# Adjacency attention followed by a graph attention layer: when the second layer's steps are issued among the first layer's beats

## The chip, the cores and the metric

The kernel runs on one core of a Trainium2 chip. The time is the device time of one execution in microseconds (us); before the change it is 4539.56 us, the median of three runs (4534.59 to 4539.63). The engines are PE (matrix products), DVE (vector), ACT (activation functions), POOL (GpSimd) and SP (which only issues transfers). Each has its own queue of instructions and they meet through semaphores.

## The reference

Two layers over x of shape 8 x 2048 x 256 (batch, node, feature) and one adjacency matrix of 2048 x 2048, all in float32.

```python
# layer 0: attention in 4 heads of 64, softmax within each chunk of 256 keys
scores = einsum('bhnd,bhjcd->bhnjc', q, kc) / sqrt(64)
scores = clip(scores, -10, 10); scores = where(mask == 0, -10, scores)
ctx = einsum('bhnjc,bhjcd->bhnd', softmax(scores, axis=-1), vc)   # the 8 chunks are summed
out = layernorm_affine(ctx @ Wo.T + bo + x)
x = layernorm(x + out)
# layer 1: graph attention, one head
Wh = x @ W;  s_i = Wh @ a1;  s_j = Wh @ a2
e = where(mask | eye, leaky_relu(s_i + s_j, 0.2), -inf)
x = layernorm(x + elu(softmax(e, axis=-1) @ Wh))
```

So layer 0 needs a softmax sum for each of 8 chunks, and layer 1 of a batch needs layer 0 of all of that batch's nodes.

## The kernel before, in words

**Layer 0.** Queries are taken in blocks of 512 (4 blocks, `ib`, in each of 8 batches, `b`) and keys in chunks of 256 (8 chunks, `j`). One (b, ib, j) is a pair of beats; there are 256 pairs, 32 for each batch. A beat (`half` 0 or 1) covers 128 keys: PE makes the scores `sc` of 4 heads (line 989) in two PSUM tiles, DVE caps and masks them in place (line 1006, "the cap"), ACT takes the exponential into `e` (line 1015). One pair later PE makes the values `u` from `e` and `v` (`values`, line 895), ACT copies them to `un` (line 1049), and the softmax sums follow (`sums`, line 909): ACT copies a sum to `ds` (line 921), a transfer gathers it as `dc`, DVE takes its reciprocal (line 926), and two more transfers (`rd`, `r`) spread it over the partitions. `scaled` multiplies `un` by `r` on DVE (line 939, or 937 for the first chunk), and POOL adds it to `ctxT` (line 940). In what follows this is "the product with the reciprocal". `inverses` puts `inverse`, `spread` and `scaled` on an agenda for given beats.

**Layer 1.** For each batch and query block there are 16 steps, one for each 128 keys: ACT `low` (line 723), DVE `leaky` and `edges` (lines 727 and 732), ACT exponential (`weights`, line 736) with a running sum `acc` on POOL (line 747), and PE `product` into the PSUM tile `us` (line 757), of which there is one. After step 15 ACT copies `us` to `hx` (line 784). A step's tile `w` comes from a pool of six. 28 blocks, those of batches 0 to 6, are of this form; batch 7 runs after the main loop in a form of its own (line 772).

**Which steps run where.** Layer 1 of a batch runs beside layer 0 of the next. A generator, `prelude`, makes `Wh`, the row maxima (two half-maxima, line 442, in each pair or more) and the row `ab` for each block; `blocks_done` and `ab` decide when a block may start. When layer 1 is under way (`together`), a pair does this: in its first beat `leaky` and `edges`, then all the values, then `weights`; in its second beat `take_lows` starts new steps and `end_beat` issues the products. Steps are metered by a credit of 1.5 for each beat (1.3 in the last batch), so three start in a pair whatever block they belong to. In such pairs two transfers on POOL's queue add the `e` tiles of the second beat to those of the first (line 1043), and the sums, taken a pair later, read one set of tiles instead of two. Other pairs ("quiet") take the sums at once, over both.

**Finish pieces.** `fin` (layer 0: output projection `po`, line 361, then two layer norms and a transpose) and `fin1` (layer 1: reciprocal, ELU and layer norm) are generators that advance one piece in a beat, from the list `fins`; the k and v projections of the next batch are in it too. `prelude` is in the list `ahead`.

**Order.** Instructions are issued in the order in which the program is written, by each engine. In the second beat of a pair with layer 1, `end_beat` issues the products, a piece of `ahead`, the pieces of `fins`, and a piece of `ahead` again; then what is due on the agenda. `inverses(p, 0)` puts the reciprocal at the end of the very beat in which the sums are made, and `scaled` two beats later (three in quiet pairs). The first 32 pairs, without layer 1, use lag 1 and four.

Of the kernel before, what the change touches and what calls it, by code (L numbers as in the profile page):

```python
# [28 lines left out]
def tile_adj_attention__then__gat(  # L29
# [36 lines left out]
    B, N, F = x.shape  # L66
# [3 lines left out]
    NT = N // P  # L70
    IB = 512
    NIB = N // IB
    TPB = IB // P
    NPAIR = H // 2
    NCH = N // CHUNK
# [268 lines left out]
    fins = []  # L344
# [352 lines left out]
    total = B * NIB * NCH  # L697

    def layer1():

        for b in range(B):
            st = states[b]
            for ib in range(NIB):
                while ib not in st["ab"] or beat < st["ab"][ib][0]:
                    yield None
                mks = [mask_block(1, ib, 0, f"{b}_{ib}_0")]
                block = {"b": b, "ib": ib, "ab": st["ab"].pop(ib)[1], "wh": st["wh"], "sj": st["sj"], "mks": mks}
                for c in range(NT):
                    if c == 3:
                        mks.append(mask_block(1, ib, 1, f"{b}_{ib}_1"))  # L710
                    yield Step(block, c)

    class Step:
# [11 lines left out]
        def leaky(self):  # L725
            k, c = self.k, self.c
            nc.vector.scalar_tensor_tensor(  # L727
                self.w, k["ab"][:, 0, :], k["sj"][:, 0, c : c + 1], self.w, ALU.add, ALU.max
            )

        def edges(self):
            nc.vector.tensor_tensor(self.w, self.w, self.k["mks"][self.c // HT][:, self.c % HT, :], ALU.min)  # L732
# [78 lines left out]

    l1 = layer1()
    l1_live = True
    ahead = [prelude(b) for b in range(B - 1)] + [last_prelude(B - 1)]

    flight = {"low": [], "leaked": [], "edged": [], "weighted": []}
    kept = []
    FROM = {"leaky": "low", "edges": "leaked", "weights": "edged"}  # L820
    agenda = {}
    beat = 0
    credit = 0.0
    RATE, LAST_RATE = 1.5, 1.3

    def l1_open():
        return any(flight.values())
# [1 line left out]
    def at(when, fn):  # L829
        agenda.setdefault(when, []).append(fn)  # L830

    def take_lows(rate, most=2.0):

        nonlocal l1_live, credit
        credit = min(credit + rate, most)
        while l1_live and credit >= 1.0 and len(set(sum(flight.values(), kept))) < 6:
            s = next(l1, False)
            if s is False:
                l1_live = False
            elif s is None:  # L840
                break
            else:
                credit -= 1.0
                flight["low"].append(s)
                s.low()

    def advance(stage, to):

        for s in flight[FROM[stage]]:
            getattr(s, stage)()  # L850
        flight[to] += flight[FROM[stage]]
        flight[FROM[stage]] = []

    def weights():
        advance("weights", "weighted")

    def leaky():
        advance("leaky", "leaked")

    def edges():  # L860
        advance("edges", "edged")

    def end_beat(products, half=None):

        if beat < 2 * NIB * NCH or beat >= 2 * total:
            for fn in agenda.pop(beat, []):
                fn()
        if products:
            for s in flight["weighted"]:
                s.product()  # L870
            flight["weighted"] = []
        for gens in {None: (ahead, fins), 0: (fins,), 1: (ahead, fins, ahead)}[half] if beat < 2 * total else (fins, ahead):
            for g in list(gens):
                if next(g, g) is g:
                    gens.remove(g)
        for fn in agenda.pop(beat, []):
            fn()


    first_m0 = two.tile([P, HT, IB], I8, tag="mask0", name="mk0_0_0_0")  # L880
# [36 lines left out]
    def inverses(p, lag):  # L917


        ds = one.tile([P, IB], F32, tag="ds", name=f"ds{p['name']}")  # L920
        nc.scalar.copy(ds, p.pop("m"))  # L921
        p["dc"] = two.tile([P, IB // DH], F32, tag="dc", name=f"dc{p['name']}")
        nc.sync.dma_start(out=p["dc"], in_=ds.rearrange("(h m) (n w) -> h m n w", m=DH, n=DH)[:, 0, :, :])

        def inverse():
            nc.vector.reciprocal(p["dc"], p["dc"])  # L926
            p["rd"] = dram3.tile([H, IB], F32, tag="rd", name=f"rd{p['name']}")
            nc.sync.dma_start(out=p["rd"].rearrange("h (m w) -> (h m) w", m=DH), in_=p["dc"])

        def spread():  # L930
            p["r"] = two.tile([P, IB], F32, tag="r", name=f"r{p['name']}")
            nc.sync.dma_start(out=p["r"], in_=p["rd"].unsqueeze(1).to_broadcast([H, DH, IB]))

        def scaled():
            r2 = p["r"].unsqueeze(1).to_broadcast([P, 2, IB])
            if p["j"] == 0:
                nc.vector.tensor_mul(p["ctxT"], p["un"], r2)
            else:
                nc.vector.tensor_mul(p["un"], p["un"], r2)  # L939
                nc.gpsimd.tensor_add(p["ctxT"], p["ctxT"], p["un"])  # L940
            if p["j"] == NCH - 1:
                ctx_done[p["b"], p["ib"]] = beat
            if p["j"] == NCH - 3:
                fins.append(fin(p["b"], p["ib"], p["ctxT"]))

        at(beat + lag, inverse)
        at(beat + lag, spread)
        at(beat + (2 if p["added"] or beat >= 2 * total else 3 + lag), scaled)

    prev = None  # L950
    unsummed = []
    mk0 = {}
    for J in range(total + 1):
        b, ib, j = J // (NIB * NCH), J // NCH % NIB, J % NCH
        live = J < total
# [3 lines left out]
        for half in range(2):  # L959
            c = 2 * j + half  # L960
            if live:
# [6 lines left out]
                if c % HT == 1:  # L968
                    n = (b * NIB + ib) * 2 + c // HT + 1
                    nb, nib, nhf = n // (2 * NIB), n // 2 % NIB, n % 2  # L970
                    if 0 < nb < B:
                        mk0[nb, nib, nhf] = mask_block(0, nib, nhf, f"{nb}_{nib}_{nhf}")
            early = J < NIB * NCH
            rate = RATE if b < B - 1 else LAST_RATE
            if half == 0:
                together = prev is not None and live and l1_open()
            if not together:
                weights()
                waiting, flight["low"] = flight["low"], []
                take_lows(rate)  # L980
                new, flight["low"] = flight["low"], waiting
                leaky()
                flight["low"] = new
            scs = []
            if live:
                for hp in range(NPAIR):
# [11 lines left out]
            if half == 0:  # L998
                for p in unsummed:
                    sums(p)  # L1000
                    inverses(p, 0)
                unsummed = []
            if live:
                cap = mk[:, c % HT, :].unsqueeze(1).to_broadcast([P, 2, IB])
# [2 lines left out]
                for hp in range(NPAIR):  # L1007
# [6 lines left out]
                    )  # L1014
                    nc.scalar.activation(e, scs[hp], AF.Exp)  # L1015
                    cur["es"].append(e)
            if not together:
                edges()
            elif half == 0:
                for s in flight["low"]:  # L1020
                    s.leaky()
                    s.edges()
                flight["edged"] += flight["low"]
                flight["low"] = []
            else:
                take_lows(2 * rate, 3.5)

            if prev is not None:
                if half == 0:
                    prev["un"] = three.tile([P, 2, IB], F32, tag="un", name=f"un{prev['name']}")  # L1030
                    if not together:
                        sums(prev)
                        inverses(prev, 1 if early else 0)
                parts = (0, 1) if together and half == 0 else (half,) if not together else ()
                ms = [ps_m.tile([P, IB], F32, tag="m", name=f"u{prev['name']}_{part}") for part in parts]
                for i in range(2):
                    for part, m in zip(parts, ms):
                        values(prev, part, m, i)
                    if together and half == 0 and i == 1:


                        for hp in range(NPAIR):
                            nc.gpsimd.dma_start(  # L1043
                                out=prev["es"][hp], in_=prev["es"][NPAIR + hp], accum_op=ALU.add
                            )
                        prev["added"] = True
                        unsummed.append(prev)
                for part, m in zip(parts, ms):
                    nc.scalar.copy(prev["un"][:, part, :], m)  # L1049
            if together and half == 0:  # L1050
                weights()

            end_beat(half == 1 or not together, half if together else None)
            if half == 1:

                if live and j == NCH - 2 and J + 2 < total:
# [5 lines left out]
        prev = cur if live else None  # L1062

    while agenda or fins or ahead or l1_live or l1_open():
        weights()
        waiting, flight["low"] = flight["low"], []
        take_lows(1.0)
        new, flight["low"] = flight["low"], waiting
        leaky()
        flight["low"] = new  # L1070
        edges()
        end_beat(True)
        beat += 1


# [42 lines left out]
```

## Time and profile before

| | |
|---|---|
| median of three runs | 4539.56 us |
| the profiled execution | 4546.43 us, of which the span of instructions is 4544.3 us |
| busy PE, DVE, ACT, POOL | 3998.4, 3357.3, 2586.8, 2019.7 us |
| scores on PE (line 989) | 1090.6 us busy, mean 645 ns, x4096 |
| caps on DVE (line 1006) | 1205.1 us busy, mean 1220 ns, x1024 |
| layer 1 products on PE (line 757) | 858.5 us busy, mean 395 ns, x3584 |
| granted PE clock | 0.958 of full speed |

One matrix product in float32 appears as two records, so 4096 records of scores are 2048 products. Busy times of overlapping records count once. A wait is given as the engine that idled, the line that it idled before, and what ended the idle time. Waits of PE's weight loads (PEld) and of its matmuls (PE) for one thing are the same wait seen twice.

### The profile page before, as it was taken

The numbers are of one execution on the slowest core, as the hardware profiler recorded it, in microseconds if no ns is written. First come the engines' busy times: TensorE is split into PE (matmuls) and PEld (weight loads), VectorE is DVE, ScalarE is ACT, GpSimd is POOL, SyncE is SP. The second block draws the span as 40 slices with busy tenths as digits, with TensorE's granted clock in tenths as the row PEclk, the third lists the DMA queues.
The fourth block names the chain that finished last, engine by engine and source line by source line (L and its number), as shares of the span: only waits on it lengthen the run. The fifth ranks groups of instructions, "written<-read, shape, count | busy, mean of one in ns | idle before, by whom it ended". The sixth has DMA issues, their size and how long they took to land. (4 is left out here: it accounts for less than half of the span.)

```text
span 4544.3 us, 59493 instructions
## 1 busy us (share of the span) xinstructions
PE 3998.4 (88%) x21845; PEld 1897.5 (42%) x21845; DVE 3357.3 (74%) x4530; ACT 2586.8 (57%) x3842; POOL 2019.7 (44%) x1203
## 2 busy tenths in 40 slices
PE   9889988899889988899888988989888998888667
PEld 3223334453344433454334543445434444244446
DVE  5876578766788657886578775886768866787777
ACT  5555556565555655665556654556655665555446
POOL 0222335554356433655346553555525554355520
PEclk9999999999999999999999999999999999999889
DMA  5554235553455434654356543555435654455521
GB/s 161 180 166 134 77 113 129 132 130 104 136 133 140 115 105 124 156 131 107 105 129 154 141 93 108 142 145 138 103 107 133 152 133 108 135 138 130 150 75 56
DMA packets 301125, 573.86 MB, mean 126 GB/s; under 512 B 90273, under 2 KB 125345, under 8 KB 299937
## 3 DMA queue, kind: packets, MB, share of 16 engines
q1 hardware_dynamic: 257344, 411.71, 29.8%
q0 software_dynamic: 43488, 158.35, 18.3%
q8 instruction: 171, 2.80, 0.3%
q14 instruction: 122, 0.99, 0.1%
HBM read 340.66 MB, written 68.88 MB: 90 GB/s over the span
## 5 line engine op out<-in xcount | busy, mean ns | idle before, releaser
L1006 DVE SCALAR_TENSOR_TENSOR sc<-sc,mk 128x1024 f32<-128x1024 f32 x1024 | 1205.1, 1220 | 560.7 <-PE sc L989 529.2
L1015 ACT ACTIVATE e<-sc 128x1024 f32<-128x1024 f32 x1024 | 1033.5, 1024 | 849.2 <-DVE sc L1006 810.3
L989 PE MATMUL sc<-qT,kT 64*128 64x512 f32 x4096 | 1090.6, 645 | 173.0 <-ACT e L1015 172.3
L757 PE MATMUL us<-wh,w 128*128 128x256 f32 x3584 | 858.5, 395 | 157.9 <-ACT hx L784 87.4
L895 PE MATMUL u<-e,v 128*32 128x512 f32 x8192 | 965.9, 596 | 26.1 <-ACT ds L921 26.0
L940 POOL TENSOR_TENSOR ctxT<-ctxT,un 128x1024 f32<-128x1024 f32 x224 | 559.8, 2499 | 853.3 <-DVE un L939 832.0
L757 PEld LDWEIGHTS us<-wh,w 128*128 128x128 f32 x3584 | 682.7, 195 | 387.8 <-ACT w L736 171.3
L747 POOL TENSOR_TENSOR acc<-acc,w 128x512 f32<-128x512 f32 x392 | 612.1, 1561 | 195.6 <-ACT w L736 178.4
L989 PEld LDWEIGHTS sc<-qT,kT 64*128 64x128 f32 x4096 | 353.3, 192 | 763.2 <-ACT e L1015 386.7
L1043 POOL DMA_DIRECT2D e<-e x302 | 269.1, 1032 | 873.2 <-PE u L895 707.2
L895 PEld LDWEIGHTS u<-e,v 128*32 128x32 f32 x8192 | 239.0, 110 | 694.5 <-issue 499.4
L727 DVE SCALAR_TENSOR_TENSOR w<-ab,sj,w 128x512 f32<-128x512 f32 x512 | 449.3, 878 | 4.4 <-ACT w L723 4.4
L732 DVE TENSOR_TENSOR w<-w,mk 128x512 f32<-128x512 f32 x512 | 431.6, 844 | 22.5 <-DMA mk<-mask 5.5
L736 ACT ACTIVATE w<-w 128x512 f32<-128x512 f32 x512 | 306.7, 629 | 209.3 <-DVE w L732 208.0
L442 DVE CUSTOM_DVE_ANT_0 fb<-sj_row,fb 128x1024 bf16<-128x1024 f32 x240 | 402.0, 1694 | 22.5 <-DMA fb<-far 22.4
L909 PE MATMUL s<-e,ones 128*32 128x512 f32 x2888 | 371.8, 616 | 0.0
L921 ACT COPY ds<-s 128x512 f32<-128x512 f32 x256 | 148.8, 581 | 383.6 <-issue 246.3
L1049 ACT COPY un<-u 128x512 f32<-128x512 f32 x512 | 295.7, 586 | 93.9 <-PE u L895 86.7
L723 ACT ACTIVATE w<-ab,sj 128x512 f32<-128x512 f32 x512 | 336.1, 711 | 1.4 <-DMA ab<-ab_d 1.4
L939 DVE TENSOR_TENSOR un<-un,r 128x1024 f32<-128x1024 f32 x224 | 308.8, 1379 | 4.0 <-DMA r<-rd 4.0
L926 DVE RECIPROCAL dc<-dc 128x16 f32<-128x16 f32 x256 | 61.9, 244 | 224.7 <-DMA dc<-ds 173.4
L909 PEld LDWEIGHTS s<-e,ones 128*32 128x32 f32 x2888 | 70.0, 111 | 280.3 <-issue 247.8
(113 smaller groups left out, 3272.7 us busy)
## 6 DMA issues: line engine op xcount, KB each, us to landing
e<-e POOLq DMA_DIRECT2D x302, 512.0 KB, 6.4
r<-rd SPq DMA_DIRECT2D x256, 256.0 KB
mk<-mask SPq DMA_DIRECT2D x120, 512.0 KB
fb<-far SPq DMA_DIRECT2D x240, 256.0 KB
xT_k<-in_xT_dram SPq DMA_DIRECT2D x32, 512.0 KB
raw<-in_adjT_dram SPq DMA_DIRECT2D x32, 512.0 KB
rawf<-in_adj_dram SPq DMA_DIRECT2D x32, 512.0 KB
x<-in_x_dram SPq DMA_DIRECT2D x32, 512.0 KB
```

The source lines that it names most:

```text
L442: nc.vector.tensor_tensor_reduce(out=fb, in0=row, in1=fb, scale=1.0, scalar=2 * FAR * 0.999, op0=ALU.add, op1=ALU.max, accum_out=dst,)
L723: nc.scalar.activation(self.w, k["ab"][:, 1, :], AF.Identity, bias=k["sj"][:, 1, c : c + 1])
L727: nc.vector.scalar_tensor_tensor(self.w, k["ab"][:, 0, :], k["sj"][:, 0, c : c + 1], self.w, ALU.add, ALU.max)
L732: nc.vector.tensor_tensor(self.w, self.w, self.k["mks"][self.c // HT][:, self.c % HT, :], ALU.min)
L747: nc.gpsimd.tensor_add(k["acc"], k["acc"], self.w)
L757: nc.tensor.matmul(k["us"][:, t, :], self.w[:, ts(t, P)], k["wh"][c // TPB][:, c % TPB, 0:F], start=(first and t % 2 == 0), stop=last, ski ...
L895: nc.tensor.matmul(m[h * DH : (h + 1) * DH, :], p["v"][pc // TPB][:, pc % TPB, f0 : f0 + DH], p["es"][2 * i + h // 2][:, h % 2, :], start= ...
L909: nc.tensor.matmul(m[h * DH : (h + 1) * DH, :], ones[:, 0:DH], p["es"][2 * i + h // 2][:, h % 2, :], start=(i == 0), stop=(i == tiles - 1),)
L940: nc.gpsimd.tensor_add(p["ctxT"], p["ctxT"], p["un"])
L989: nc.tensor.matmul(sc[:, h, :], kTs[b][c // TPB][h * D : (h + 1) * D, hp, ts(c % TPB, P)], qT[h * D : (h + 1) * D, hp, :], start=True, sto ...
L1006: nc.vector.scalar_tensor_tensor(scs[hp], scs[hp], -CLIP, cap, ALU.max, ALU.min)
L1015: nc.scalar.activation(e, scs[hp], AF.Exp)
```

## The change

It alters when things are issued, not what is computed. (1) Steps of layer 1 start in groups given by `GROUPS`, of 3, 3, 3, 3, 2 and 2, one group in a pair, and no group reaches into the next block. The credit is gone; a batch of 64 steps takes 24 pairs. In the main loop steps start only in the second beat of a pair, in quiet pairs too. (2) Reciprocals have a lag of one beat, and `scaled` comes three beats after the sums (four where both tiles were summed). (3) In the second beat of a pair with layer 1, `end_beat` first issues what is due (now the reciprocal and `scaled`), then the finish pieces, then the products, then two pieces of `ahead`.

```diff
+    GROUPS = (3, 6, 9, 12, 14, NT)
...
-    def take_lows(rate, most=2.0):
-
-        nonlocal l1_live, credit
-        credit = min(credit + rate, most)
-        while l1_live and credit >= 1.0 and len(set(sum(flight.values(), kept))) < 6:
+    def take_lows(group):
+
+        nonlocal l1_live, next_c
+        end = next(n for n in GROUPS if n > next_c) if group else next_c + 1
+        while l1_live and next_c < end and len(set(sum(flight.values(), kept))) < 6:
...
-                credit -= 1.0
+                next_c += 1
                 flight["low"].append(s)
                 s.low()
...
+    def step_of_layer1():
+        weights()
+        steps, flight["low"] = flight["low"], []
+        take_lows(False)
+        leaky_and_edges(steps)
...
-    def end_beat(products, half=None):
-
-        if beat < 2 * NIB * NCH or beat >= 2 * total:
-            for fn in agenda.pop(beat, []):
-                fn()
-        if products:
-            for s in flight["weighted"]:
-                s.product()
-            flight["weighted"] = []
-        for gens in {None: (ahead, fins), 0: (fins,), 1: (ahead, fins, ahead)}[half] if beat < 2 * total else (fins, ahead):
...
+    def end_beat(half):
+
+
+        if beat < 2 * NIB * NCH or beat >= 2 * total or half == 1:
+            due()
+        if half is None:
+            products()
+            for gens in (ahead, fins) if beat < 2 * total else (fins, ahead):
+                pieces(gens)
+        elif half == 0:
+            pieces(fins)
+        else:
+            pieces(fins)
+            products()
+            pieces(ahead)
+            pieces(ahead)
+        due()
...
-        at(beat + (2 if p["added"] or beat >= 2 * total else 3 + lag), scaled)
+        at(beat + (2 if not lag else 3 if p["added"] else 4), scaled)
...
-            if not together:
-                weights()
-                waiting, flight["low"] = flight["low"], []
-                take_lows(rate)
-                new, flight["low"] = flight["low"], waiting
-                leaky()
-                flight["low"] = new
+            if not live:
+                step_of_layer1()
...
-                    inverses(p, 0)
+                    inverses(p, 1 if live else 0)
...
-            if not together:
-                edges()
-            elif half == 0:
-                for s in flight["low"]:
-                    s.leaky()
-                    s.edges()
-                flight["edged"] += flight["low"]
-                flight["low"] = []
-            else:
-                take_lows(2 * rate, 3.5)
+            if live and half == 0:
+                steps, flight["low"] = flight["low"], []
+                leaky_and_edges(steps)
+            elif live:
+                take_lows(True)
...
-                        inverses(prev, 1 if early else 0)
+                        inverses(prev, 1 if live else 0)
```

After the main loop one step starts in each beat, as before.

More of the change, by code (lines that the diff above doesn't have):

```diff
@@ L816, in tile_adj_attention__then__gat @@
     ahead = [prelude(b) for b in range(B - 1)] + [last_prelude(B - 1)]
-    flight = {"low": [], "leaked": [], "edged": [], "weighted": []}
+    flight = {"low": [], "edged": [], "weighted": []}
     kept = []
-    FROM = {"leaky": "low", "edges": "leaked", "weights": "edged"}
+    next_c = 0
     agenda = {}
     beat = 0
-    credit = 0.0
-    RATE, LAST_RATE = 1.5, 1.3
     def l1_open():
@@ L842, in take_lows, with leaky_and_edges, due, pieces @@
             else:
-                credit -= 1.0
+                next_c += 1
                 flight["low"].append(s)
                 s.low()
[L847 to L852, printed above, removed]
-    def weights():
[L855 to L861, printed above, removed]
-    def end_beat(products, half=None):
-        if beat < 2 * NIB * NCH or beat >= 2 * total:
-            for fn in agenda.pop(beat, []):
-                fn()
-        if products:
-            for s in flight["weighted"]:
-                s.product()
-            flight["weighted"] = []
-        for gens in {None: (ahead, fins), 0: (fins,), 1: (ahead, fins, ahead)}[half] if beat < 2 * total else (fins, ahead):
-            for g in list(gens):
-                if next(g, g) is g:
-                    gens.remove(g)
+        next_c %= NT
+    def leaky_and_edges(steps):
+        for s in steps:
+            s.leaky()
+            s.edges()
+        flight["edged"] += steps
+    def weights():
+        for s in flight["edged"]:
+            s.weights()
+        flight["weighted"] += flight["edged"]
+        flight["edged"] = []
+    def step_of_layer1():
[3 more added lines that the diff above has]
+        leaky_and_edges(steps)
+    def due():
         for fn in agenda.pop(beat, []):
             fn()
+    def pieces(gens):
+        for g in list(gens):
+            if next(g, g) is g:
+                gens.remove(g)
+    def products():
+        for s in flight["weighted"]:
+            s.product()
+        flight["weighted"] = []
+    def end_beat(half):
[13 more added lines that the diff above has]
+        due()
     first_m0 = two.tile([P, HT, IB], I8, tag="mask0", name="mk0_0_0_0")
@@ L972, in tile_adj_attention__then__gat @@
                         mk0[nb, nib, nhf] = mask_block(0, nib, nhf, f"{nb}_{nib}_{nhf}")
-            early = J < NIB * NCH
-            rate = RATE if b < B - 1 else LAST_RATE
             if half == 0:
                 together = prev is not None and live and l1_open()
-            if not together:
-                weights()
-                waiting, flight["low"] = flight["low"], []
-                take_lows(rate)
-                new, flight["low"] = flight["low"], waiting
-                leaky()
-                flight["low"] = new
+            if not live:
+                step_of_layer1()
             scs = []
@@ L1051, in tile_adj_attention__then__gat @@
                 weights()
-            end_beat(half == 1 or not together, half if together else None)
+            end_beat(half if together else None)
             if half == 1:
@@ L1064, in tile_adj_attention__then__gat @@
     while agenda or fins or ahead or l1_live or l1_open():
[L1065 to L1072, printed above, removed]
+        step_of_layer1()
+        end_beat(None)
         beat += 1
```

## The prediction

> **What bounds the kernel now.** I read the page's busy times first, then the same by stage, then the waits, then single pairs of beats. In the page, the engines:
>
> ```profile
> PE 3998.4 (88%) x21845; PEld 1897.5 (42%) x21845; DVE 3357.3 (74%) x4530; ACT 2586.8 (57%) x3842; POOL 2019.7 (44%) x1203
> ```
>
> One batch, cut by stage (columns: us; PE, weight loads, DVE, ACT, POOL busy; granted clock; DMA share; GB/s). First the end of the previous batch's layer 1 (pairs 0 to 5 of 32), then the quiet pairs 6 to 15, then pairs 16 to 31 with layer 1:
>
> ```profile
> 2053.00:2161.00 108.00, 97.73 (x522) 50.77 (x520) 80.03 (x101) 61.79 (x91) 62.20 (x40) 0.95 0.47 104
> 2161.00:2315.00 154.00, 133.65 (x776) 48.78 (x774) 89.33 (x132) 81.00 (x122) 42.66 (x20) 0.96 0.38 114
> 2315.00:2603.00 288.00, 262.78 (x1421) 135.61 (x1419) 241.78 (x314) 176.68 (x265) 166.69 (x105) 0.99 0.58 140
> ```
>
> PE is the bound everywhere, idle for 10.3 + 20.4 + 25.2 = 56 us of 550. In the last stage DVE is at 84%, close behind: it has no PE stall's worth of room in every pair. So the change can only pay through PE's idle time, about 56 us a batch, or through PE work it removes. The waits name the idle time (us in total, times, longest):
>
> ```profile
> ACT e L1015 <- DVE sc L1006: 810.3, 362, 8.6
> PEld sc L989 <- ACT e L1015: 386.7, 294, 8.1
> DVE dc L926 <- DMA dc<-ds: 173.4, 52, 9.8
> PE us L757 <- ACT hx L784: 87.4, 14, 9.9
> PE po L361 <- POOL ctxT L940: 33.1, 13, 4.2
> ```
>
> The fourth is the plainest. Steps go three to a pair and a block has 16, so in each batch two block ends fall inside a group: steps 14, 15 and the next block's 0, then 15, 0, 1. The product of step 0 needs the one PSUM tile us, which ACT still has to copy to hx. The timeline of one such pair (start, length, idle before):
>
> ```profile
> 2401.77 3.72 PE L757 MATMUL us<-wh,w 128*128 128x256 f32 x16 [0.36 <-ACT w L736]
> 2401.85 1.77 DVE L727 SCALAR_TENSOR_TENSOR w<-ab,sj,w 128x512 f32<-128x512 f32 x1
> 2407.57 2.34 DVE L1006 SCALAR_TENSOR_TENSOR sc<-sc,mk 128x1024 f32<-128x1024 f32 x2
> 2408.81 2.15 ACT L1015 ACTIVATE e<-sc 128x1024 f32<-128x1024 f32 x2 [2.85 <-DVE sc L1006]
> 2412.70 0.99 ACT L784 COPY hx<-us 128x1024 f32<-128x1024 f32 x1
> 2413.74 3.78 PE L757 MATMUL us<-wh,w 128*128 128x256 f32 x8 [8.25 <-ACT hx L784]
> ```
>
> PE is idle for 8.25 us. The copy is late because ACT does the exponentials and three lows first, and those wait for a cap (L1006) that DVE reaches only at 2407.57, behind two batch statistics, a product (L939) and a reciprocal. A quiet pair shows the other stall:
>
> ```profile
> 2249.06 0.57 SPq L923 DMA_DIRECT2D dc<-ds  x1
> 2253.43 0.25 DVE L926 RECIPROCAL dc<-dc 128x16 f32<-128x16 f32 x1 [5.87 <-DMA dc<-ds]
> 2253.60 2.34 DVE L1006 SCALAR_TENSOR_TENSOR sc<-sc,mk 128x1024 f32<-128x1024 f32 x2
> 2255.92 3.21 PE L989 MATMUL sc<-qT,kT 64*128 64x512 f32 x8 [3.52 <-ACT e L1015]
> ```
>
> DVE waits 5.87 us for a small transfer with the next cap queued behind it, and PE loses 3.52 us.
>
> [...] scores freed by 2411 waited on PE behind the stalled product until 2417.46. [...] L727 takes 0.74 us alone and 1.77 us beside a POOL acc; L939 1.21 and 2.31. [...] for dc on SyncE's queue the trace has more, 4.4 us from issue at 2249.06 to the reciprocal at 2253.43.
>
> **The change part by part.** Following the loop's counters with before's rules gives 151 pairs with layer 1, which the page's 302 e<-e transfers confirm. The new rules give 161: pairs 16 to 31 and 0 to 7 of each batch, from pair 15 in the last. The start doesn't slip: the next prelude waits for blocks_done (pair 7 instead of 5), and its ab is still ready for pair 16. 82 steps are left for after the loop in both.
>
> 1. Groups that end with their block. No product of step 0 follows a product of step 15 in its beat; a whole pair lies between, and the copy (1.01 us) hides under the next scores. Of PE's 87.4 us I don't count all: in the pair shown, PE would go on to the next scores, which need the second cap and its exponentials. Those were ready at about 2411 instead of 2405.5; one step fewer (1.43 us at least, 3.4 us as contended) and L939 and L926 behind the cap (1.44 us) bring them to 2406 to 2408. So up to 2.5 of 8.25 us stays. Recovered: 0.7 x 87.4 = 61 us; bounds 20 (DVE late everywhere) and 87.
>
> 2. Ten pairs more with layer 1. Sums there take 8 matmul records instead of 16 (1.06 against 1.92 us), the halves being added by DMA: 10 x 0.9 = 9 us of PE. The steps themselves only move. 108 pairs have three steps and 53 two, where DVE has 1.4 us less.
>
> 3. Reciprocals a beat later. Adding up the stretches with neither matmul nor weight load in the quiet pairs of batches 1 to 6, PE's idle time before scores that wait for an exponential is 61.6 us; DVE there waits 187 us for dc. With lag 1 the transfer has a beat (7 us) instead of none. What remains are other causes, such as a far tile at pair 13. I take two thirds: 41 us; bounds 15 and 61. If that cover were gone the 4.4 us would stand before a cap again, as today. SyncE's rd and r follow, ahead of the finish pieces' transfers of that beat; r's wait for rd holds that queue about 2 us, and mask loads are issued before it.
>
> 4. Products a beat later (L939, then POOL's ctxT add). They leave the first beat of a pair, where DVE does two caps (2.34 us), three steps (4.3) and statistics, for the second, with caps, L939 (1.38), reciprocal and two half-maxima (2 x 1.70). PE in the first beat has 2.0 + 1.06 + 3.72 = 6.8 us, in the second 2.0 + 5.4 = 7.4 us. So DVE has 6.6 against 6.8 and 7.4 against 7.4 before statistics, where it had 8.3 against 6.8. PE's idle before scores in layer-1 pairs is 57 us, plus 23 in the last batch. I take 15 us back; bounds 40 back and 40 lost, since those two beats have no slack left. The buffer un (three) is released half a pair later: ACT's copy comes about 10 us after the product (3.4 us left of that beat, 6.8 to the end of the values); when POOL has the gamma product and sum (6.6 us) ahead of the ctxT add (2.4), that is just enough: I allow 0.5 us, 28 times, 14 us lost. Behind the ctxT add on POOL stand that beat's finish pieces and the next e<-e, which waits for the values of the next pair anyway (707 us in all).
>
> 5. Finish pieces ahead of products. po now falls into the first beat, after the values, more than a beat after ctxT's add. PE's 33.1 us for ctxT goes; po then waits for the un copies to free its PSUM tile (under 1 us). Net 25 us; bounds 10 and 33. DVE's waits for po (175.7 us) shrink, which I don't count again.
>
> 6. After the loop: one beat more, 292 us / 80 = 3.6 us lost.
>
> Sum: 61 + 9 + 41 + 15 - 14 + 25 - 4 = 133 us. The profiled execution took 4546.4 us (span 4544.3, 2.1 around it), 6.9 over the median. So 4546.4 - 133 = 4413 profiled, and 4539.6 - 133 = 4407 as the median.
>
> **The rivals.**
>
> A, the sum, 4407; its own range 4350 to 4470. Chance 0.53.
>
> B, the stalls change their name. DVE at 84% can't follow a PE that waits less, and PE waits for exponentials instead of hx and ctxT. Left: sums 9, quiet pairs 41, 20 of part 1 and none of 4 and 5, less 4: 66 us, 4474 us. For it speaks ACT's 810 us wait for DVE. Against it: most of DVE's own idle time in layer-1 pairs (245 of 429 us in pairs 16 to 31 and 0 to 5 of batches 1 to 6) is waiting for PE's scores. Chance 0.22.
>
> C, the bursts were the cause and PE runs nearly dense: idle falls from 56 to 22 us a batch, 34 x 6.5 = 221 us, 4319 us. Chance 0.08.
>
> D, slower: the second beat overflows on DVE. Reciprocal, L939 contended (2.31) and half-maxima back to back, contended as at 3.4 us for two or more, push the next first cap back in three-step pairs. From 133 / 108 = 1.2 us a pair it eats the gain; at 1.7 us it costs 184 us, net 51 us, 4591 us. Against it: PE has 6.8 us of work from the values of the pair before while that cap is late. Chance 0.12.
>
> E, the gains stand but the new waits match them: 4540 us. Chance 0.05.
>
> **How the numbers follow.** Faster, same and slower are within and beyond 0.2%, about 9 us, what a measurement of this kernel can tell from no change. A, B and C are faster, 0.83; E 0.05; D 0.12. The range leaves out D, E and a third of C, 0.20: 4330 to 4525.
>
> **What would show it.** Right: 322 e<-e transfers and 2808 records of s; no wait of us for hx; waits of dc near nothing, of po for ctxT too; quiet pairs (8 a batch) near 14.5 us; a batch near 530 us. B: the wait of scores for e grows in layer-1 pairs by what hx loses. D: DVE over 90% in pairs 16 to 31, and first caps late after half-maxima. Wrong altogether: the layer-1 pairs grow by more than 1.2 us each, or the granted clock (0.95 to 0.99 by stage, and no lower where PE is denser) falls.

## The result, and the profile after

The changed kernel takes 4470.33 us (median of four runs, 4452.42 to 4471.89) against 4539.6 us: the ratio is 0.9841, with a 95% interval of 0.9815 to 0.9867. That is 69 us faster, a little over half of the 133 us forecast, and inside the range. The profiled execution took 4469.18 us, against 4546.43.

The engines in the page of the changed kernel:

```profile
PE 3999.9 (90%) x21765; PEld 1914.8 (43%) x21765; DVE 3328.3 (75%) x4530; ACT 2587.5 (58%) x3842; POOL 2018.1 (45%) x1223
...
e<-e POOLq DMA_DIRECT2D x322, 512.0 KB, 6.9
```

PE's busy time hasn't moved (3998.4 before), so the 77 us between the two spans are all idle time of PE. The 322 transfers are the 161 pairs that the counters gave. The same batch as before by stage (columns: us; PE, weight loads, DVE, ACT, POOL busy; clock; DMA share; GB/s): pairs 0 to 7 with layer 1, quiet pairs 8 to 15, pairs 16 to 31.

```profile
2014.00:2137.60 123.60, 121.02 (x674) 60.57 (x672) 90.82 (x124) 84.30 (x125) 74.60 (x50) 0.99 0.54 129
2137.60:2261.50 123.90, 106.34 (x628) 41.91 (x626) 75.90 (x114) 64.71 (x99) 33.06 (x15) 0.96 0.38 119
2261.50:2553.00 291.50, 267.76 (x1397) 136.65 (x1395) 235.91 (x308) 169.57 (x253) 163.40 (x103) 0.96 0.57 139
```

The batch takes 539 us instead of 550. Pairs 0 to 7 are nearly dense (PE idle for 2.6 us), but the last stage still has 23.7 us without a matmul, as before (25.2), with 44 steps in it instead of 47. PE's busy time there even rose by 5 us (262.8 to 267.8), at a granted clock of 0.96 instead of 0.99; the last section comes back to that. The waits of the changed kernel (us in total, times, longest):

```profile
PE sc L1001 <- ACT e L1027: 119.7, 70, 6.3
...
PE pk L255 <- ACT un L1056: 52.0, 18, 6.1
...
DVE dc L945 <- DMA dc<-ds: 34.7, 27, 4.2
...
PE pt L387 <- ACT y L330: 30.6, 30, 6.1
...
PE s L928 <- DMA e<-e: 21.6, 19, 2.4
...
PE po L361 <- POOL ctxT L959: 11.6, 1, 11.6
```

What the change aimed at is gone: no product waits for hx, the waits for dc fell from 173 to 35 us and those of po for ctxT from 33 to 12. But three waits that cost 4 us together before now cost 104: the key projection pk for un, the transposes pt for ACT's y, and the sums s for the added e tiles. (Lines have moved: scores 989 to 1001, caps 1006 to 1018, exponentials 1015 to 1027, values 895 to 914, sums 909 to 928, `un` 1049 to 1056, `dc` 926 to 945, `ctxT` 940 to 959.) One wait of pk in the timeline of the changed kernel (start, length, idle before):

```profile
2428.57 3.41 POOL L959 TENSOR_TENSOR ctxT<-ctxT,un 128x1024 f32<-128x1024 f32 x1
...
2429.69 3.37 DVE L442 CUSTOM_DVE_ANT_0 fb<-sj_row,fb 128x1024 bf16<-128x1024 f32 x1
...
2432.99 2.35 DVE L1018 SCALAR_TENSOR_TENSOR sc<-sc,mk 128x1024 f32<-128x1024 f32 x2
...
2434.25 2.15 ACT L1027 ACTIVATE e<-sc 128x1024 f32<-128x1024 f32 x2 [6.05 <-DVE sc L1018]
...
2436.30 1.07 ACT L1056 COPY un<-u 128x512 f32<-128x512 f32 x2
...
2436.93 2.07 PE L255 MATMUL pk<-xT_k,WT_k 128*128 128x512 f32 x2 [5.90 <-ACT un L1056]
```

This is a whole chain in six lines. POOL's ctxT add, which the change moved here, runs beside the second half-maximum, which takes 3.37 us instead of 1.2. The first cap of the next pair stands behind it on DVE, the exponentials wait for the cap, the copies to un stand behind the exponentials on ACT, and pk needs the PSUM tiles that the copies free. The same stall, 5.8 to 6.1 us, stands in pair 26 of each of batches 1 to 6 and makes 35 of pk's 52 us. In batches 5 and 6 it is another DVE instruction beside the same add that runs long, line 320 on `rstd_c`, 2.31 and 1.87 us instead of 0.17.

### The profile page after: what moved, and what is told of

Same layout as the page of the kernel before. It is cut to its first block, busy times and chain, and to the rows that moved or that the text cites. A ratio compares the mean times of both kernels' runs of the same rounds, so it can differ in the third digit from the quotient of the medians.

```text
span 4467.4 us, 59396 instructions
## 1 busy us (share of the span) xinstructions
PE 3999.9 (90%) x21765; PEld 1914.8 (43%) x21765; DVE 3328.3 (75%) x4530; ACT 2587.5 (58%) x3842; POOL 2018.1 (45%) x1223
## 5 line engine op out<-in xcount | busy, mean ns | idle before, releaser
L1001 PE MATMUL sc<-qT,kT 64*128 64x512 f32 x4096 | 1067.6, 635 | 120.2 <-ACT e L1027 119.7
L914 PE MATMUL u<-e,v 128*32 128x512 f32 x8192 | 981.3, 599 | 16.9 <-ACT ds L940 14.6
L959 POOL TENSOR_TENSOR ctxT<-ctxT,un 128x1024 f32<-128x1024 f32 x224 | 581.5, 2596 | 869.4 <-DVE un L958 844.1
L747 POOL TENSOR_TENSOR acc<-acc,w 128x512 f32<-128x512 f32 x392 | 565.9, 1444 | 241.1 <-ACT w L736 224.2
L1050 POOL DMA_DIRECT2D e<-e x322 | 287.6, 1032 | 703.6 <-PE u L914 679.3
L732 DVE TENSOR_TENSOR w<-w,mk 128x512 f32<-128x512 f32 x512 | 410.7, 802 | 21.1 <-DMA mk<-mask 3.6
L442 DVE CUSTOM_DVE_ANT_0 fb<-sj_row,fb 128x1024 bf16<-128x1024 f32 x240 | 407.3, 1723 | 14.5 <-DMA fb<-far 14.5
L928 PE MATMUL s<-e,ones 128*32 128x512 f32 x2808 | 373.8, 608 | 21.6 <-DMA e<-e 21.6
L255 PE MATMUL pk<-xT_k,WT_k 128*128 128x512 f32 x256 | 138.5, 691 | 58.8 <-ACT un L1056 52.0
```

Source lines behind the costliest of these rows:

```text
L442: nc.vector.tensor_tensor_reduce(out=fb, in0=row, in1=fb, scale=1.0, scalar=2 * FAR * 0.999, op0=ALU.add, op1=ALU.max, accum_out=dst,)
L747: nc.gpsimd.tensor_add(k["acc"], k["acc"], self.w)
L914: nc.tensor.matmul(m[h * DH : (h + 1) * DH, :], p["v"][pc // TPB][:, pc % TPB, f0 : f0 + DH], p["es"][2 * i + h // 2][:, h % 2, :], start= ...
L928: nc.tensor.matmul(m[h * DH : (h + 1) * DH, :], ones[:, 0:DH], p["es"][2 * i + h // 2][:, h % 2, :], start=(i == 0), stop=(i == tiles - 1),)
L1001: nc.tensor.matmul(sc[:, h, :], kTs[b][c // TPB][h * D : (h + 1) * D, hp, ts(c % TPB, P)], qT[h * D : (h + 1) * D, hp, :], start=True, sto ...
```

## The experiments

The change has three parts: the groups, the later reciprocals with the later products, and the order of pieces. The first runs undo each, or do one alone. Two theories stood against each other: A, the groups carry the gain and parts add up; B, stalls change their name and the later reciprocals carry the gain. In the later runs A and B are the two that the text of that run names.

**Without the groups** (steps three to a pair, across block ends):

```diff
-        end = next(n for n in GROUPS if n > next_c) if group else next_c + 1
+        end = next_c + (3 if group else 1)
```

> The changed kernel with groups of three that cross the ends of blocks, everything else kept. Theory A (the groups carry the gain, because PE's 87 us before products for hx are truly freed): these waits come back and the time is about 4530 us. Theory B (the wait only changes its name, the later reciprocals carry the gain): about 4490 us, with waits of us for hx again and fewer waits of scores for e. The forecast's part 1 (61 us) and part 2 (9 us) would give 4540 us.

Measured: 4584.31 us, ratio 1.0112 (1.0079 to 1.0146), 1.1% slower than before the change. Neither number was near.

```profile
PE us L757 <- ACT hx L784: 106.8, 14, 10.0
...
PE pab L465 <- DVE m L461: 60.6, 17, 10.1
...
PE po L361 <- POOL ctxT L959: 47.9, 7, 9.3
```

The waits for hx are back and longer, as A said, and two more appear: the two pieces of `ahead` now follow each other, and a transpose pab waits on PE for a maximum that DVE hasn't reached. Beside the lag and the new order the groups are worth some 120 us (1.0112 to 0.9841). A run below shows that most of this is harm that the new order does without them.

**Without the lag** (reciprocals and products as before):

```diff
-        at(beat + (2 if not lag else 3 if p["added"] else 4), scaled)
+        at(beat + (2 if p["added"] or beat >= 2 * total else 3 + lag), scaled)
...
-                    inverses(p, 1 if live else 0)
+                    inverses(p, 0)
...
-                        inverses(prev, 1 if live else 0)
+                        inverses(prev, 1 if J < NIB * NCH else 0)
```

> The changed kernel with reciprocals at the end of the beat of their sums and the products two beats after them (three in quiet pairs), as before. Theory A: the later product overloads DVE's second beat by about what the later reciprocal saves in quiet pairs, so about 4470 to 4485 us; DVE's waits for dc come back, PE's waits of pk for un go. Theory B: 4511 us or more (the forecast's 41 us of part 3 are lost).

Measured: 4529.98 us, ratio 0.9997 (0.9988 to 1.0006): the whole gain is gone. B. DVE waits 179 us for dc again, and po waits 100 us for ctxT, since the new order puts it ahead of the products while the product with the reciprocal is early.

**With the old order** (products, ahead, finish pieces, ahead):

```diff
-            pieces(fins)
             products()
             pieces(ahead)
+            pieces(fins)
             pieces(ahead)
```

> The changed kernel with the old order at the end of the second beat: products, a piece of ahead, the finish pieces, a piece of ahead. Theory A: with po in the first beat already, the order is worth little: 4465 to 4480 us; the transposes' waits for ACT's y (about 31 us) go. Theory B, as the forecast had it: 25 us are lost, 4495 us.

Measured: 4465.98 us, ratio 0.9845 (0.9816 to 0.9875). The order is worth nothing beside the other two parts. The transposes' wait for y went, and pr's for un came (33 us).

**The groups alone** (both of the last two edits):

> The groups alone: old lags and old order. Theory A: 4480 to 4490 us, most of the gain. Theory B: about 4525 us, a fifth of it.

Measured: 4517.93 us, ratio 0.9965 (0.9952 to 0.9977). B: no product waits for hx, and of 87 us some 16 are left. The waits of this kernel say where the rest went:

```profile
DVE dc L945 <- DMA dc<-ds: 178.9, 48, 9.8
...
PE us L757 <- ACT w L736: 94.8, 62, 16.4
...
PE pw L402 <- ACT wh L403: 46.0, 6, 9.4
```

Products wait more for their weights (94.8 us, before the change 69.8), and in pair 7, the last with layer 1 of a batch, the pieces of the next prelude (pw) wait some 9 us for ACT, which waits for a cap that DVE reaches only after 9.27 us before dc.

**The lag alone**, on the kernel before, with what is due issued first in the second beat:

```diff
-        if beat < 2 * NIB * NCH or beat >= 2 * total:
+        if beat < 2 * NIB * NCH or beat >= 2 * total or half == 1:
...
-        at(beat + (2 if p["added"] or beat >= 2 * total else 3 + lag), scaled)
+        at(beat + (2 if not lag else 3 if p["added"] else 4), scaled)
...
-                    inverses(p, 0)
+                    inverses(p, 1 if live else 0)
...
-                        inverses(prev, 1 if early else 0)
+                        inverses(prev, 1 if live else 0)
```

> The kernel before with the later reciprocals and products alone (and what is due issued first in the second beat): no groups, old order of pieces. Theory A (lag and groups add up): groups alone gave 0.35%, so the lag alone should give the other 1.2%, about 4480 us. Theory B (each needs the other: with blocks that end inside a group, hx is copied still later): 4540 us or slower, PE's wait of us for hx over 87 us.

Measured: 4506.29 us, ratio 0.9931 (0.9914 to 0.9947), between the two. hx still costs 65 us. Groups alone and lag alone make 1.04%; together, in the old order, they make 1.55%, so neither hides the other's gain. In the old order, then, the groups beside the lag are worth 39 us (0.9931 to 0.9845) and not 120, and without the groups the new order costs 82 us (0.9931 to 1.0112).

**Is DVE the bound?** Half-maxima over 64 of 1024 columns, in the changed kernel and in the one before:

```diff
-            out=fb,
-            in0=row,
-            in1=fb,
+            out=fb[:, 0:64],
+            in0=row[:, 0:64],
+            in1=fb[:, 0:64],
```

> The changed kernel with half-maxima over 64 instead of 1024 columns (a part of the row maximum is left out); transfers and all else stay. DVE loses about 240 x 1.6 = 380 us of work. Theory A (DVE's second beat bounds the changed kernel's layer-1 pairs): at least 70 us faster than the changed kernel, about 4395 us, and pk's wait for un (52 us) nearly gone. Theory B (PE's own order bounds): 20 us or less, 4450 us.

> The kernel before with the same shortened half-maxima (the same part left out). Theory A: DVE matters less in the second beat there; 30 to 50 us faster than before, 4490 to 4510 us, and the wait for hx stays near 60 us. Theory B: the same 20 us or less as in the changed kernel.

Measured: 4324.08 us (ratio 0.9521, 0.9498 to 0.9545) and 4437.78 us (0.9777, 0.9762 to 0.9791). The changed kernel's page line:

```profile
PE 3946.6 (91%) x21765; PEld 1898.8 (44%) x21765; DVE 2994.7 (69%) x4530; ACT 2580.6 (60%) x3842; POOL 1927.4 (45%) x1223
```

DVE lost 334 us of work, and the kernel 146 us; the kernel before lost 312 and 102. So DVE's lateness bounds both more than either theory had it, and the changed kernel more. (POOL's busy time fell too, by 91 and 81 us; these runs don't take the two apart.) Of the 146 us PE's idle time (the span less all stretches with a matmul or a weight load) accounts for 87, from 466 to 379 us, and PE's own busy time for 53: its granted clock was 0.970 instead of 0.957. A's detail was wrong: pk's wait fell from 52 to 33 us only, so the length of the half-maxima makes only a part of it.

**The reciprocal later, the product where it was** (two beats after the sums, in the first beat):

```diff
-        at(beat + (2 if not lag else 3 if p["added"] else 4), scaled)
+        at(beat + (2 if not lag or p["added"] else 4), scaled)
```

> The changed kernel with the reciprocal still a beat later, but the product with it two beats after the sums (end of the next pair's first beat), where it was before. Theory A (the second beat overflows on DVE, and un comes free late, because of the product): 4430 to 4450 us, below the changed kernel; pk's wait for un falls. Theory B (the later product is what lets the finish pieces find ctxT ready and keeps DVE's first beat short): 4490 us or more, with po waiting for ctxT again (up to 97 us, as without any lag).

Measured: 4481.8 us, ratio 0.9864 (0.9844 to 0.9884), not told apart from the changed kernel. One wait replaced the others:

```profile
PE po L361 <- POOL ctxT L959: 108.6, 15, 8.5
...
PE pk L255 <- ACT un L1056: 15.7, 7, 3.9
```

pk's wait fell from 52 to 16 us, as A said, with the product and its ctxT add out of the second beat. But po, now ahead of the products, stands before ctxT with the products behind it. Two ways to take that away follow.

**po a beat later**, after the values:

```diff
-        while (b, ib) not in ctx_done or ctx_done[b, ib] == beat:
+        while (b, ib) not in ctx_done or beat < ctx_done[b, ib] + (2 if 2 * NIB * NCH <= beat < 2 * total else 1):
```

> The kernel of m4_product2 (reciprocal a beat later, product with it in the next pair's first beat) with the output projection po one beat later, after the values, where ctxT is ready. Theory A (the later product bought nothing but a ready ctxT, and cost a late un): PE's 105 us before po for ctxT go, pk's wait for un stays near 16 us, 4400 to 4430 us, faster than the changed kernel. Theory B (the wait changes its name again, DVE being the bound): 4465 us or more, the idle time coming back before scores, s or other pieces.

Measured: 4479.06 us, ratio 0.9855 (0.984 to 0.987). B: the wait for ctxT is gone and not one microsecond is won.

```profile
PE sc L1001 <- ACT e L1027: 168.9, 89, 6.3
...
PE pt L387 <- ACT y L330: 36.5, 33, 5.7
```

The scores' wait for exponentials rose from 107 to 169 us, the transposes' from nearly nothing to 37.

**The same with the old order:**

> The same with the products ahead of the finish pieces in the second beat. Theory A: the order is still worth little, within 10 us of n5_po_later. Theory B: the same.

Measured: 4408.51 us, ratio 0.9702 (0.9683 to 0.9722). Both expectations were wrong: here the order is worth 70 us.

**po right after the product, and the old order.** In pairs with layer 1 this is the kernel before with the groups and with the reciprocal a beat later, issued first in that beat. In quiet pairs the product with the reciprocal also comes a beat later (four after the sums, not three), as in the last three runs:

> The fourth corner of the square of po's beat and the order: groups and the later reciprocal, with the product two beats after the sums, po in the beat after it, and the products ahead of the finish pieces, all three as before the change. If the order is what counts (n6_po_later_order without the later po): 4400 to 4420 us, with PE's wait of po for ctxT under 35 us, since the products stand between. If po's later beat is what counts: 4465 to 4485 us.

Measured: 4365.9 us (4361.89 to 4373.3), ratio 0.9614 (0.9595 to 0.9633), 104 us below the changed kernel.

```profile
PE 3957.0 (91%) x21765; PEld 1877.5 (43%) x21765; DVE 3317.6 (76%) x4530; ACT 2595.9 (59%) x3842; POOL 2040.9 (47%) x1223
...
PE po L361 <- POOL ctxT L959: 20.4, 15, 2.6
...
PE s L928 <- DMA e<-e: 6.4, 10, 1.1
...
PE pk L255 <- ACT un L1056: 4.4, 8, 0.6
```

With the products of layer 1 ahead of it, po finds ctxT nearly ready; the three new waits are all but gone (no transpose waits for y).

**pk a beat later**, in the changed kernel:

```diff
-                k_beat = 4 * n - 2 if b == 0 else first + 4 * n + 4
+                k_beat = 4 * n - 2 if b == 0 else first + 4 * n + 5
```

> The changed kernel with the key projection pk one beat later, in the second beat (and the value projection in the first beat after it), so that pk no longer follows the values. Theory A (pk's 52 us wait is made by un, whose buffer comes free late or whose copy stands behind late exponentials, and is pk's alone): 4430 us. Theory B (DVE is late there, so whatever PE has next waits as long): 4460 to 4475 us, the wait now before scores for e or before pv for un.

Measured: 4468.08 us, ratio 0.982 (0.9799 to 0.984), the changed kernel's within the intervals. B:

```profile
PE sc L1001 <- ACT e L1027: 148.9, 76, 6.3
...
PE pr L599 <- POOL ctxT L959: 19.3, 5, 4.7
```

pk's wait is gone, and scores (119.7 to 148.9 us) and pr wait in its place; PE's idle time is 464 us, where it was 466. The 52 us named what PE had next while DVE, ACT and POOL were late.

The runs in one table, each against runs of the kernel before on its own chip; idle time of PE and clock are those of the profiled execution. An "old" product beside a later reciprocal is old in pairs with layer 1 only:

| groups | reciprocal | product | order | po | ratio | PE idle, us | clock |
|---|---|---|---|---|---|---|---|
| no | old | old | old | old | 1 | 544 | 0.958 |
| yes | old | old | old | old | 0.9965 | 530 | 0.958 |
| no | later | later | old | follows | 0.9931 | 499 | 0.954 |
| yes | old | old | new | old | 0.9997 | 533 | 0.950 |
| no | later | later | new | follows | 1.0112 | 558 | 0.946 |
| yes | later | later | new | follows | 0.9841 | 466 | 0.957 |
| yes | later | later | old | follows | 0.9845 | 473 | 0.960 |
| yes | later | old | new | old | 0.9864 | 483 | 0.954 |
| yes | later | old | new | a beat later | 0.9855 | 482 | 0.959 |
| yes | later | old | old | a beat later | 0.9702 | 437 | 0.962 |
| yes | later | old | old | old | 0.9614 | 407 | 0.971 |

A fourth tile for un wasn't tried. Why the order costs 70 us with an early product and a late po, and nothing with a late product, is not settled: in the first case the waits of pt for y go and those of the scores fall (169 to 136 us), in the second the waits of u for ds and of pr for un come instead.

## Why the prediction was right or wrong

The direction, the pairs (161) and the range were right. The time was rival B's (4474 us) rather than A's: stalls came back under other names. Parts 1 and 2 together were priced at 70 us, 3 and 4 at 42 and 5 at 25. Added in the old order, one after the other, the groups gave 16 us (0.9965), the later reciprocals and products 54 more (0.9845), and the new order 2 (0.9841); with the lag first it gave 31 and the groups 39. So most of what is missing was priced on the groups and the order. That the time still fell inside A's range is partly luck: in 3 and 4 a gain far beyond one bound met a loss far beyond the other.

**Part 1, groups, 61 us.** The mechanism held, no product waits for hx. The size did not: alone the groups gave 16 us, below the lower bound of 20. I had priced where PE goes on to, the next scores, but only in one pair; the freed time was met by late weights, by pw in pair 7 and by DVE before dc. With the later reciprocals and products they gave 39 us.

**Part 2, 9 us of PE work.** 80 records of s went, as forecast (2808). PE's busy time didn't fall, not even that of the sums alone (371.8 us before, 373.8 after), and PE stood before late e<-e adds for another 21.6 us, where it had not waited at all. What filled the 9 us in the busy time is not shown.

**Part 3, later reciprocals, 41 us.** The worst-sized term. With groups and the old order, the reciprocal a beat later (and in quiet pairs the product with it) takes 0.9965 to 0.9614, some 159 us; the bound was 61. In the new order, where po stands before ctxT in both kernels, the same step gives 60 us (0.9997 to 0.9864). I had counted only PE's idle time before scores in quiet pairs (61.6 us) as what could be won. In the old order PE's idle time falls by 123 us (530 to 407). Adding up the traces pair by pair, quiet pairs make 62 of them, my whole bound, and pairs with layer 1 make 60, where I had counted none and where nothing but the reciprocal moved. The other 31 us between the spans are PE's busy time, at a clock of 0.971 instead of 0.958.

**Part 4, later products, 15 gained and 14 lost.** Here the sign failed. In the old order the later product costs 0.9614 to 0.9845, 105 us, beyond the 40 bounded; in the new order it makes no difference that can be told. My count of DVE's beats (7.4 against PE's 7.4 us in the second) left out statistics and contention, which the six lines above show (a half-maximum of 3.37 us beside POOL's ctxT add, where the one just before it took 1.21). That is rival D's mechanism, first caps late after half-maxima, at work in a kernel that is still faster; D's other mark is missing, as DVE is at 81% in pairs 16 to 31, not over 90%. The un buffer was my 14 us; ACT waits for POOL's ctxT before un for 27.8 us, where it was 5.0.

**Part 5, order, 25 us.** It gave 0.9845 to 0.9841, nothing, and in no setting tried did it gain. With the product early it costs 0.9614 to 0.9864, 114 us; po then waits before the products instead of behind them (108.6 against 20.4 us). The wait of 33 us before the change was already short: products were its cover, as the kernel with the ratio 0.9614 shows with 20 us.

**Part 6** can't be told apart: the stretch after the loop took 292 and 290 us.

**Rivals.** B had the size and the cause, a DVE that can't follow. Its own mark failed, since the scores' wait for e fell in layer-1 pairs too (60 to 42 us); the time went to pk, pt and s. My case against B, that DVE idles 245 us for PE's scores there, was wrong as an argument: an engine that idles on average can be late in each burst, and shortened half-maxima gave 146 us. Quiet pairs took 15.5 us, where I expected 14.5, and so no less than before (15.4): the first of them is some 26 us long.

## What to carry to other kernels

Price a removed wait by asking what each engine would wait for next, and try the parts of a change in combination: beside the groups and the later reciprocal, the later product and the order cost 105 and 114 us, and 103 together. A part's worth is only its worth beside the others: the groups gave 16, 39 or 123 us. Take a wait out of the queue that the most others stand behind (a reciprocal of 0.25 us on DVE) before a long wait of the bound engine; here, in the old order, the two gave 159 and 16 us. In an in-order queue, put a piece that must wait behind work that is ready, not ahead of it: behind the products of layer 1 po waited 20.4 us for ctxT, ahead of them 108.6 us.

## What was not expected of the hardware

The granted clock differs between kernels that do nearly the same matmuls, and stays with the kernel over its runs: 0.943 to 0.948 in the changed kernel without its groups, 0.956 to 0.961 in the changed kernel, 0.970 to 0.971 in the fastest (the kernel before had 0.954 to 0.961 on all chips). It isn't lower where PE is denser; the two densest kernels (PE idle for 379 and 407 us) have the highest (0.970 and 0.971 in their profiles).

What sets it is not shown. In the traces' records it is either full or half: half for 382 us before the change (in 71 stretches), 388 us in the changed kernel (67) and 256 us in the fastest (47). That stalls of PE bring it about is my estimate, from the stalls that follow. One is the wait of pk shown above. Before pk begins and while it runs (columns: us; PE, weight loads, DVE, ACT, POOL busy; clock; DMA share; GB/s):

```profile
2432.40:2435.80 3.40, 0.00 (x0) 0.00 (x0) 3.40 (x5) 1.45 (x2) 3.33 (x3) 1.00 0.52 144
2435.80:2442.60 6.80, 5.67 (x7) 2.50 (x8) 3.39 (x5) 3.41 (x6) 2.52 (x2) 0.50 0.72 140
```

PE did nothing in the first stretch, and had half the clock in the second: the eight records of pk took 6.50 us together, where eight take 3.8 us on average in the fastest kernel (120.1 us for 256; before the change 121.2). Over the 6.5 us from pk's start, the clock was 0.56 to 0.75 after all six of these stalls in pair 26. The prediction's own lines had it too: after the stall of 8.25 us before hx, eight records of us took 3.78 us, where sixteen had taken 3.72; the clock from 2413.7 to 2418 was 0.57. I priced only the idle time.

So these stalls cost their length and then slower matmuls behind them. Of the 102 us between the spans of the changed kernel and the fastest, idle time of PE makes 59 and busy time 43 (4001 to 3958 us, a weight load or a matmul running), with the same 21765 matmul records. In the stretches at half clock PE was busy for 293 us in the changed kernel and for 186 in the fastest; half of the difference, what full clock would save there by my estimate, is 53 us, enough for the 43. The median record is the same in both, 592 ns for u and 589 for sc. It is worked out from the busy times and clocks of the two traces; no run changed the clock alone.
